# Two banded gating layers on one core: inverse roots a step later, output statistics spread over the steps, and part of the norm's columns on VectorE

## The chip, the cores and the metric

The kernel runs on one core of a Trainium2 chip. The core has TensorE (PE; PEld is its loading of weights), VectorE (DVE), ScalarE (ACT), GpSimd (POOL) and SyncE (SP), each with an instruction queue of its own that runs in order. [...] The metric is the time of one execution on the device in microseconds, median of several.

## The reference, cut to what matters

The input x is 512 x 512 positions of 64 channels. Two layers of the same form follow each other.

```python
def layer(x):
    v = gn(x)                                   # 32 groups, over all positions
    xn = ln(v)                                  # over the 64 channels
    left  = (xn @ Wl + bl) * mask * sigmoid(xn @ Wlg + blg)      # 64 -> 128
    right = (xn @ Wr + br) * mask * sigmoid(xn @ Wrg + brg)      # 64 -> 128
    gate  = sigmoid(xn @ Wog + bog)                              # 64 -> 128
    # out[i, j, h] = sum over |d| <= 4 of left[i + d, i, h] * right[i + d, j, h]
    out = banded(left, right, 4)
    out = ln(out, out_norm_scale, out_norm_bias) * gate          # over the 128 channels
    return x + out @ Wo + bo
x = layer_0(x); x = layer_1(x)
```

Everything is float32. Both layer norms need a mean and an inverse root for every one of the 262,144 positions. Two of them matter here: the norm of the input (64 channels) and the norm of the banded product, here called the output norm (128 channels).

## The kernel before, in words

**Tiling.** The rows i are cut into nine blocks of 64 rows that overlap by 8, the columns j into two halves of 256. A block and a pair of column stretches of 128 (one of each half) is a chunk, so a layer has 18 chunks. The 128 partitions hold 64 rows of one half and 64 of the other. A chunk is cut into sixteen units of eight columns (`JU = 8`, `NU = 16`), and the program advances by **steps**, one unit a step. `layer` writes out the order by hand: each engine gets its instructions in program order, step after step, and there is no planner at run time.

**What one step t issues.** In this order: the loads of later units' z tiles, the fetch of the next output unit's residual (`fetch`, tile XR), slabs of the left factor (`take_left`, tile A) and the recall of a stored transposed unit (`recall`, tile zg), all on SyncE's DMA queue; up to three output statistics; the affine of the group norm on a unit some seven to nine steps ahead (`affine`, two GpSimd instructions on z; VectorE does it for the first units of a layer); the first half of the right factor (`right`: TensorE into PSUM, sigmoid on ScalarE, product on VectorE into RO); up to two more statistics; the output gates (`gates`); the second half of `right`; the norm of the input of unit t + 2 on GpSimd (`inner_norm`, two instructions on z); `turned` (TensorE transposes of the normed output `on`, then two VectorE instructions that add a bias, multiply by the gate and write ZH); the transposes of z for unit t + 1 (`transposed`, `kept`); the bias on the residual on GpSimd (`biased`); the remaining output statistics; the input statistics of the unit whose affine was a step ago (`inner_stats`, four bn_stats); the last product with Wo, its addition to XR on VectorE and the store (`end`); in layer one sums for the next group norm; then, every fourth step, the solve; then the output norm of the next step's unit (`norm`); last the band products of the step (`mix`).

**RO.** One tile in SBUF, `[128, 64, 240, 2]`, holds the right factor and, once a `mix` has passed over it, the banded product in its place. A band product takes eight channels of a chunk (TensorE into two PSUM banks, one half copied back by ScalarE and one by VectorE). A chunk has sixteen of them, spread over ten steps, those with t % 16 from 0 to 9, one or two in each. Steps 10 to 15 have none.

**Statistics and solve.** `out_stats` is one VectorE `bn_stats` over two columns of RO; a unit has four. They can only start when the chunk's last band product is back, so from step 10 on. `looks` says at which step the four of a unit are issued, all four in the same step. In step t with `t % 4 == 3`, `solve` gathers the input statistics of four units and the output statistics of up to four: five small VectorE instructions (var, nm, a first guess of the inverse root by integer arithmetic, rs), then ten small GpSimd instructions (`rsqrt`) and two more that make the scale `rs` and the bias `nm` of the output norm. Ahead of the solve GpSimd gets the affines of the next step (`then_affine`), so that it has them to do while VectorE makes its part.

**Norm.** `norm` is eight ScalarE activations, one for each column of a unit, `on = RO * rs + nm` with a scale and a bias for each partition. The tile `on` has one buffer. The first output unit of a chunk is normed in step 13, the next in step 14 and so on, sixteen in a row.

**Buffers.** z has twelve, `ps2` (two banks each) two, `sg` two, XR four. The table `count` says how many units' affines go into each of the sixteen steps, and `ahead` follows from it; a unit's load is issued two steps before its affine, its statistics one step after.

Instructions issued through the in-order wrappers (`en.vector` and so on) all have one line in the profile, L362, so their tiles tell them apart.

Of the kernel before, what the change touches and what calls it, by code (L numbers as in the profile page):

```python
# [10 lines left out]
AF = mybir.ActivationFunctionType  # L11
ALU = mybir.AluOpType
# [10 lines left out]
JU = 8  # L23
JQ = 4
NU = JC // JU
# [54 lines left out]
def tile_two_banded_layers(  # L80
# [7 lines left out]
    _, L, _, D = x.shape  # L88
# [326 lines left out]
    def affine(u: Unit, engine):  # L415

        engine.tensor_tensor(u.z, u.z, mid(ga, JU), ALU.mult)
        engine.tensor_tensor(u.z, u.z, mid(gb, JU), ALU.add)
# [97 lines left out]
    def take_left(n: int, h: int) -> bass.AP:  # L516


        A = lp.tile([P, S, HA], F32, tag="A", name="A")
        at = n * size + h * slab + WIN * HA  # L520
        for e in range(2):
            en.sync.dma_start(
                A[e * S : (e + 1) * S].rearrange("p i h -> p (i h)"),
                strided(left_of, at, ((S + 2 * WIN) * HA, S), (1, S * HA)),
            )
        return A
# [33 lines left out]
    def out_stats(o: Out, st: bass.AP, k: int):  # L560
        en.vector.bn_stats(
            st[:, k, :],
            RO[:, :, o.c + 2 * k : o.c + 2 * k + 2, :].rearrange("p h j t -> p h t j"),
        )
# [31 lines left out]
            for n, o in enumerate(outs):  # L596
                o.rs, o.nm = ro[:, n * JU : (n + 1) * JU], nm[:, n * JU : (n + 1) * JU]

    def norm(o: Out):
        o.on = onp.tile([P, JU, H], F32, tag="on", name="on")  # L600
        for j in range(JU):
            en.scalar.activation(
                o.on[:, j, :].rearrange("p (h t) -> p h t", t=2), RO[:, :, o.c + j, :],
                AF.Identity, bias=o.nm[:, j : j + 1], scale=o.rs[:, j : j + 1],
            )

    def recall(o: Out):
        o.t = ztg.tile([P, JU // 2, P], F32, tag="zg", name="zg")
        en.sync.dma_start(o.t, later[o.at])
# [41 lines left out]
    def fetch(src: bass.AP, o: Out, w: dict, n: int):  # L651
        o.n, o.xr = n, XR[n % len(XR)]
        for e in range(2):
            en.sync.dma_start(o.xr[e * S : e * S + o.blk.m, :, 1 : 1 + 2 * D], rows_of(src, o, e))
# [38 lines left out]
    def layer(src: bass.AP, dst: bass.AP, w: dict, stats: bool, then=None):  # L693
        per = LH // JC
        n_chunks = len(blocks) * per
        LAG = NU + 14
        own = NU - JW // JU
        units, outs, lefts, mixes, looks, slabs = {}, {}, {}, {}, {}, {}
        free = NA * [NU - 2]
        for c in range(n_chunks):  # L700
            b, t0 = blocks[c // per], (c + 1) * NU
            for k in range(NU):
                t = c * NU + k
                units[t] = u = Unit(t, blk=b, j=c % per * JC + k * JU)
                j = k * JU if c % 2 == 0 else (JC + k * JU if k < own else JC - JW + (k - own) * JU)
                u.c = j

            for f in range(NU):
                o = outs[c * NU + LAG + f] = Out(
                    b, units[c * NU + (f + own) % NU], c % per * JC + f * JU  # L710
                )
                looks.setdefault(t0 + (8 + f if f > 3 else 10 + f // 2), []).append(o)

            step = [t0 + n for n, k in enumerate((2, 1, 2, 2, 1, 2, 1, 2, 2, 1)) for _ in range(k)]
            for n, t in enumerate(step):
                mixes.setdefault(t, []).append((c, n * HB))

            for h in range(H // HA):
                slabs.setdefault(free[-NA], []).append((c, h))
                free.append(step[(h + 1) * (HA // HB) - 1] + 1)  # L720
        for n in range(0, NEAR * JQ, JU):
            t = 3 + n // JU * 2
            lefts[t] = Unit(t, near=n)
        first_t, last_t = min(outs), max(outs)

        def inputs(t: int) -> list:
            return [d[t] for d in (units, lefts) if t in d]

        loads, affines, inners = {}, {}, {}
        count = [1, 1, 2, 1, 1, 1, 2, 1, 1, 1, 1, 0, 1, 1, 1, 0]
        ahead = {}
        done = -5 - NU
        for t in range(-7 - NU, n_chunks * NU):
            for _ in range(count[t % NU]):
                ahead[done + 7] = t
                done += 1
        for t in range(n_chunks * NU):
            for u in inputs(t):  # L740
                loads.setdefault(ahead[t] - 2, []).append(u)
                affines.setdefault(ahead[t], []).append(u)
                inners.setdefault(ahead[t] + 1, []).append((t, u))

        early = [u for t in sorted(loads) for u in loads[t] if u.near is None and u.at < 7]
        for u in early:
            load(src, u)
        yield
        A, sti, sto, then_affine = {}, {}, None, []
        for t in range(min(loads), last_t + 3):  # L750
            if then and t == max(units) + 2:
                then()
            for u in loads.get(t, []):
                if u not in early:
                    load(src, u)
            if t + 1 in outs:
                fetch(src, outs[t + 1], w, t + 1)
            for c, h in slabs.get(t, []):
                A[c, h] = take_left(c // per, h)
            if t + 2 in outs:  # L760
                recall(outs[t + 2])

            looking = []
            for o in looks.get(t, []):
                if sto is None:
                    sto = sm.tile([P, NB // 2, 6], F32, tag="sto", name="sto"), []
                st, os = sto
                n = len(os) * (JU // 2)
                looking += [(o, st[:, n : n + JU // 2, :], k) for k in range(JU // 2)]
                os.append(o)  # L770

            for v in looking[:3]:
                out_stats(*v)

            for u in affines.pop(t, []):
                affine(u, en.vector if u.at < NU + 4 else en.gpsimd)
            if t % 4 == 3 and t > NU:
                then_affine = affines.pop(t + 1, [])

            todo = []  # L780
            for at, u in inners.get(t, []):
                key = (at + 2) // 4
                if key not in sti:
                    sti[key] = sm.tile([P, 3 * NB // 4, 6], F32, tag="sti", name="sti", bufs=3), []
                st, us = sti[key]
                n = len(us) * (JU // 2)
                u.mean = st[:, n : n + JU // 2, 1::3]
                todo += [(u, st[:, n : n + JU // 2, :], k) for k in range(JU // 2)]
                us.append(u)

            if t in units:
                right(units[t], 0, w)
            for v in looking[3:5]:
                out_stats(*v)
            if t in outs:
                gates(outs[t], w)
            if t in units:
                right(units[t], JQ, w)
            if t in lefts:
                for q in range(0, min(JU, NEAR * JQ - lefts[t].near), JQ):  # L800
                    left(lefts[t], q, w)
            for u in inputs(t + 2):
                inner_norm(u)
            if t in outs:
                turned(outs[t], w)
            for u in inputs(t + 1):
                transposed(u)
                kept(u)
            if t in outs:
                biased(outs[t], w, stats)  # L810
            for v in looking[5:]:
                out_stats(*v)
            for v in todo:
                inner_stats(*v)
            if t - 1 in outs:
                end(dst, outs[t - 1], w)
            if stats and t - 2 in outs:
                sums(outs[t - 2], t - 2 == first_t, t - 2 == last_t)
            if t % 4 == 3:
                st, us = sti.pop((t + 5) // 4, (None, []))  # L820
                so, os = sto or (None, [])
                sto = None
                for u in then_affine:
                    affine(u, en.gpsimd)
                then_affine = []
                if us or os:
                    solve(w, us, os, st, so)
            if t + 1 in outs:
                norm(outs[t + 1])
            for n, (c, h0) in enumerate(mixes.get(t, [])):  # L830
                mix(c, A[c, h0 // HA], h0)

# [69 lines left out]
    RO = keep.tile([P, H // 2, 2 * JC - JW, 2], F32, name="RO")  # L902
# [58 lines left out]
```

## Time and profile before

| | us |
|---|---|
| median of 3 runs | 5036.04 |
| lowest, highest | 5017.72, 5038.81 |
| profiled execution, its own time | 5033.71 |
| its span, first to last instruction | 5031.9 |

| engine | busy us | share of the span |
|---|---|---|
| TensorE, products | 4211.9 | 84% |
| TensorE, weight loads | 3564.2 | 71% |
| VectorE | 3875.7 | 77% |
| ScalarE | 3636.6 | 72% |
| GpSimd | 3827.9 | 76% |

The mean granted clock of TensorE was 0.963 of full speed. The costliest single group is the output norm on ScalarE: 4608 activations `on<-RO,nm,rs`, 1868.6 us busy. The DMA queues moved 982.32 MB, 195 GB/s over the span.

How to read what follows: an instruction is named by what it writes and reads (`RO<-banks,sg`). In a timeline a row has start, length, engine, line, operation, names, shape. In a table of windows a row has the window, its length, the busy time of each engine (with the number of instructions), the granted clock, the share of busy DMA engines and GB/s. In a view by tile a row has minimum, median and maximum length in ns.

### The profile page before, as it was taken

What the parts mean: (1) busy time and instruction counts of PE and PEld (TensorE: products, weight loads), DVE (VectorE), ACT (ScalarE), POOL (GpSimd) and SP (SyncE); (2) the same over time, 40 slices, a digit from 0 to 9 for tenths busy, and PEclk for the clock granted to TensorE, in tenths of its full rate; (3) what the DMA queues carried; (4) which work ended last, traced back from release to release, by engine and by line L of the source; (5) the groups of instructions that cost most, each with busy time, mean ns of one, the idle gap of its engine ahead of it and who ended that gap; (6) DMA issues with size and microseconds to landing.
All of it is one profiled execution on the core that took longest, in us unless ns stands there. A gap on an engine that the chain in (4) does not pass through costs nothing. (4 is left out here: it accounts for less than half of the span.)

```text
span 5031.9 us, 173294 instructions
## 1 busy us (share of the span) xinstructions
PE 4211.9 (84%) x67090; PEld 3564.2 (71%) x67090; DVE 3875.7 (77%) x9661; ACT 3636.6 (72%) x8156; POOL 3827.9 (76%) x4739
## 2 busy tenths in 40 slices
PE   1026899999999999999984589999999999998998
PEld 0024788888888888888863477777777777777776
DVE  6774778888888888888766478888888888888877
ACT  0013688888888888888883268888888888888888
POOL 0036888888888888888734688888888888888863
PEclk9988999999999999999997899999999999999999
DMA  7914677767776776777663457777777777777766
GB/s 316 406 57 120 172 200 200 204 197 200 203 199 199 198 201 198 198 199 205 190 168 95 118 172 199 203 202 201 199 205 201 202 202 202 204 204 202 206 186 173
DMA packets 905343, 982.32 MB, mean 195 GB/s; under 512 B 114210, under 2 KB 641608, under 8 KB 900168
## 3 DMA queue, kind: packets, MB, share of 16 engines
q1 hardware_dynamic: 897248, 948.49, 65.2%
q10 hardware_dynamic: 7272, 22.73, 1.1%
q8 instruction: 531, 8.70, 0.8%
q14 instruction: 292, 2.39, 0.2%
HBM read 658.42 MB, written 312.46 MB: 193 GB/s over the span
## 5 line engine op out<-in xcount | busy, mean ns | idle before, releaser
L362 ACT ACTIVATE on<-RO,nm,rs 128x128 f32<-128x128 f32 x4608 | 1868.6, 495 | 13.2 <-PE bank L362 12.7
L362 PE MATMUL banks<-pack,zT 64*128 64x256 f32 x9360 | 1322.6, 404 | 128.9 <-ACT zT L362 56.2
L362 PEld LDWEIGHTS banks<-pack,zT 64*128 64x128 f32 x9360 | 884.9, 194 | 493.7 <-DVE RO L362 200.8
L362 PE MATMUL banks<-RO,A 64*64 64x128 f32 x18432 | 1169.4, 279 | 14.4 <-ACT zT L362 14.4
L362 PEld LDWEIGHTS banks<-RO,A 64*64 64x64 f32 x18432 | 1097.4, 184 | 41.3 <-ACT zT L362 17.2
L362 DVE TENSOR_TENSOR RO<-banks,sg 128x512 f32<-128x512 f32 x1152 | 787.8, 684 | 347.6 <-ACT sg L362 331.5
L362 ACT ACTIVATE sg<-banks 128x512 f32<-128x512 f32 (+1 forms) x1188 | 694.7, 587 | 364.1 <-PE banks L362 254.3
L362 DVE COPY RO<-banks 128x512 f32<-128x512 f32 x576 | 397.9, 691 | 592.8 <-ACT RO L362 592.8
L362 DVE BATCH_NORM_STATS2 sto<-RO 128x6 f32<-128x256 f32 x2304 | 847.1, 414 | 1.2
L362 DVE SCALAR_TENSOR_TENSOR ZH<-bank,pack,gate 128x448 f32<-128x448 f32 (+1 forms) x1152 | 738.7, 683 | 51.3 <-ACT gate L362 39.5
L362 POOL TENSOR_TENSOR z<-z,gb 128x512 f32<-128x512 f32 x536 | 686.6, 1281 | 42.0
L362 PE MATMUL bank<-pack,ZH 128*64 128x64 f32 x18432 | 689.4, 230 | 5.6 <-ACT gate L362 5.2
L362 POOL TENSOR_TENSOR z<-z,ga 128x512 f32<-128x512 f32 x536 | 688.5, 1284 | 0.1
L362 POOL TENSOR_TENSOR z<-z,rs 128x512 f32<-128x512 f32 x586 | 616.1, 1051 | 46.0
L362 PEld LDWEIGHTS bank<-pack,ZH 128*64 128x64 f32 x18432 | 608.0, 142 | 47.8 <-ACT gate L362 9.2
L362 POOL TENSOR_TENSOR z<-z,sti 128x512 f32<-128x512 f32 x586 | 623.1, 1063 | 0.0
L362 ACT ACTIVATE gate<-bank 128x448 f32<-128x448 f32 (+1 forms) x1152 | 566.2, 544 | 73.1 <-PE bank L362 63.0
L362 PE MATMUL bank<-zg,pack 64*128 64x448 f32 (+1 forms) x2304 | 551.7, 550 | 1.2 <-DMA zg<-later 0.8
L362 ACT COPY RO<-banks 128x512 f32<-128x512 f32 x576 | 335.7, 583 | 299.2 <-PE banks L362 299.2
L362 PEld LDWEIGHTS bank<-ident,on 64*128 64x128 f32 x9216 | 402.6, 139 | 210.1 <-ACT gate L362 97.2
L362 POOL TENSOR_TENSOR XR<-XR,pack 120x512 f32<-120x512 f32 (+1 forms) x352 | 418.7, 1191 | 135.2 <-DMA XR<-in_x_dram 50.4
L362 PE MATMUL bank<-ident,on 64*128 64x64 f32 x9216 | 443.2, 225 | 86.3 <-ACT gate L362 59.3
(140 smaller groups left out, 3756.7 us busy)
## 6 DMA issues: line engine op xcount, KB each, us to landing
later<-zT SPq DMA_DIRECT2D x576, 256.0 KB
A<-left_of SPq DMA_DIRECT2D x576, 256.0 KB
zg<-later SPq DMA_DIRECT2D x576, 256.0 KB
z<-in_x_dram SPq DMA_DIRECT2D x576, 128.0 KB
z<-mid_x SPq DMA_DIRECT2D x576, 128.0 KB
gn_x<-in_x_dram SPq DMA_DIRECT2D x16, 4096.0 KB
XR<-in_x_dram SPq DMA_DIRECT2D x448, 112.0 KB
mid_x<-XR SPq DMA_DIRECT2D x448, 112.0 KB
```

The costliest lines, as they stand in the source:

```text
L362: return lambda *a, **k: tc.keep_in_program_order(f(*a, **k))
```

## The change

Five things change, all in the order of `layer` but one.

1. `norm` takes a number of columns that VectorE does, with one `tensor_scalar` each (multiply by `rs`, add `nm`, both one value for each partition). It is 2 in steps 13 and 14 of sixteen, 3 in step 15, and 0 in the others.
2. `looks` no longer puts a unit's four output statistics into one step. Before, steps 10 to 25 (counted from a chunk's first band product) had 8, 8, 4, 4, 4, 4, then 4 in each of eight steps, and none in the last two. Now they have 5, 5, 6, 3, 3, 3, 7, then 4 in each of eight.
3. The solve comes in steps with `t % 4 == 0` and not 3. The keys that group input units go with it, and so does the early issue of the next step's affines.
4. `count`, the affines in each of sixteen steps, becomes 1, 1, 2, 1, 2, 1, 1, 2, 1, 1, 1, 0, 1, 1, 0, 0 (before: 1, 1, 2, 1, 1, 1, 2, 1, 1, 1, 1, 0, 1, 1, 1, 0), and the plan starts one unit further ahead.
5. In a layer's first sixteen steps each has one affine.

```diff
-    def norm(o: Out):
+    def norm(o: Out, on_vector: int):
+
         o.on = onp.tile([P, JU, H], F32, tag="on", name="on")
         for j in range(JU):
-            en.scalar.activation(
-                o.on[:, j, :].rearrange("p (h t) -> p h t", t=2), RO[:, :, o.c + j, :],
-                AF.Identity, bias=o.nm[:, j : j + 1], scale=o.rs[:, j : j + 1],
-            )
+            to = o.on[:, j, :].rearrange("p (h t) -> p h t", t=2)
+            of = RO[:, :, o.c + j, :]
+            nm, rs = o.nm[:, j : j + 1], o.rs[:, j : j + 1]
+            if j < JU - on_vector:
+                en.scalar.activation(to, of, AF.Identity, bias=nm, scale=rs)
+            else:
+                en.vector.tensor_scalar(to, of, rs, nm, ALU.mult, ALU.add)
...
+        look = [n for n, k in zip(range(10, 25), (5, 5, 6, 3, 3, 3, 7) + 8 * (4,)) for _ in range(k)]
...
-                looks.setdefault(t0 + (8 + f if f > 3 else 10 + f // 2), []).append(o)
+                for k in range(JU // 2):
+                    looks.setdefault(t0 + look[f * (JU // 2) + k], []).append((o, k))
...
-        count = [1, 1, 2, 1, 1, 1, 2, 1, 1, 1, 1, 0, 1, 1, 1, 0]
+        count = [1, 1, 2, 1, 2, 1, 1, 2, 1, 1, 1, 0, 1, 1, 0, 0]
         ahead = {}
-        done = -5 - NU
+        done = -4 - NU
         for t in range(-7 - NU, n_chunks * NU):
-            for _ in range(count[t % NU]):
+            for _ in range(1 if 0 <= t < NU else count[t % NU]):
                 ahead[done + 7] = t
                 done += 1
...
-            for o in looks.get(t, []):
+            for o, k in looks.get(t, []):
                 if sto is None:
                     sto = sm.tile([P, NB // 2, 6], F32, tag="sto", name="sto"), []
                 st, os = sto
-                n = len(os) * (JU // 2)
-                looking += [(o, st[:, n : n + JU // 2, :], k) for k in range(JU // 2)]
-                os.append(o)
+                if k == 0:
+                    os.append(o)
+                n = (len(os) - 1) * (JU // 2)
+                looking.append((o, st[:, n : n + JU // 2, :], k))
...
-            if t % 4 == 3 and t > NU:
+            if t % 4 == 0 and t > NU:
                 then_affine = affines.pop(t + 1, [])
...
-                key = (at + 2) // 4
+                key = (at + 1) // 4
...
-            if t % 4 == 3:
-                st, us = sti.pop((t + 5) // 4, (None, []))
+            if t % 4 == 0:
+                st, us = sti.pop((t + 4) // 4, (None, []))
...
-                norm(outs[t + 1])
+
+                norm(outs[t + 1], {13: 2, 14: 2, 15: 3}.get(t % NU, 0))
```

## The prediction

> **What bounds the kernel now.** I read the page's busy row first. No engine is full over the span, so the bound changes with the step.
>
> ```profile
> PE 4211.9 (84%) x67090; PEld 3564.2 (71%) x67090; DVE 3875.7 (77%) x9661; ACT 3636.6 (72%) x8156; POOL 3827.9 (76%) x4739
> ```
>
> Next I cut one chunk of sixteen steps at the ends of its steps: window k runs from the last ZH instruction of step k-1 to the last one of step k. These are windows 11, 12, 13, 14, 15, 0 and 1 of a chunk in layer one; the columns are length, busy time of TensorE, weight loads, VectorE, ScalarE and GpSimd, then the granted clock and DMA.
>
> ```profile
> 1502.43:1508.80 6.37, 5.66 (x96) 4.41 (x94) 6.37 (x18) 5.55 (x14) 3.69 (x3) 1.00 0.85 246
> 1508.80:1515.49 6.69, 5.32 (x94) 4.09 (x90) 6.66 (x22) 5.20 (x13) 2.86 (x10) 1.00 0.71 206
> 1515.49:1521.47 5.98, 5.54 (x98) 4.58 (x98) 4.48 (x10) 5.84 (x15) 5.67 (x8) 1.00 0.81 237
> 1521.47:1527.15 5.68, 5.23 (x95) 4.29 (x93) 5.27 (x14) 5.54 (x14) 5.52 (x6) 1.00 0.35 101
> 1527.15:1532.84 5.69, 5.25 (x96) 4.31 (x94) 5.27 (x15) 5.56 (x15) 5.53 (x6) 1.00 0.82 243
> 1532.84:1541.22 8.38, 5.13 (x70) 4.12 (x67) 8.35 (x18) 5.00 (x12) 7.33 (x14) 0.87 0.79 235
> 1541.22:1551.79 10.57, 10.57 (x188) 9.66 (x188) 5.86 (x12) 7.45 (x18) 10.18 (x12) 0.94 0.64 179
> ```
>
> See the full column of each row: VectorE in 11 and 12, ScalarE (with GpSimd) in 13, 14 and 15, VectorE in 0, TensorE in 1. Windows 2 to 10, with band products, are TensorE's (for example 7.14 busy of 7.14). Only windows 11 to 1 can gain much; over 30 chunks they average 6.4, 6.7, 6.1, 5.65, 5.6, 7.9, 10.4 us, and a chunk takes about 122 us.
>
> Why is window 0 long? The timeline at the end of step 15 shows it.
>
> ```profile
> 1410.67 1.19 POOL L362 TENSOR_TENSOR XR<-XR,fewer 120x512 f32<-120x512 f32 x1
> 1411.18 0.72 DVE L362 TENSOR_SCALAR var<-sti 128x32 f32<-128x32 f32 x1
> 1411.81 1.27 POOL L362 TENSOR_TENSOR z<-z,ga 128x512 f32<-128x512 f32 x1
> 1411.82 1.31 DVE L362 SCALAR_TENSOR_TENSOR var<-sto,pack 128x32 f32<-128x32 f32 x1
> 1413.17 0.18 DVE L362 TENSOR_SCALAR var<-var 128x32 f32<-128x32 f32 x1
> 1413.26 1.25 DVE L362 TENSOR_SCALAR nm<-sto 128x32 f32<-128x32 f32 x1
> ```
>
> The small instructions of the solve, 0.18 us elsewhere, end when a GpSimd instruction ends. Over the kernel:
>
> ```profile
> L362 DVE TENSOR_SCALAR nm<-sto x144: 167/176/1255, 538.2 to 5003.2; 128x32 f32<-128x32 f32 x144
> ```
>
> The maximum is 1.255 us against a median of 0.176. In the chunks of layer one the five solve instructions hold VectorE 2.76 us in window 0 and 0.6 us after steps 3, 7 and 11, where GpSimd already sits waiting for them. VectorE's next evacuation is late, TensorE cannot get its PSUM banks, and then runs at half clock for a while:
>
> ```profile
> 1416.30:1419.67 3.37, 3.34 (x57) 3.18 (x57) 2.64 (x5) 2.61 (x7) 2.77 (x9) 0.52 0.70 216
> 931.21:940.42 9.21, 9.21 (x162) 8.37 (x162) 5.76 (x12) 7.13 (x17) 8.57 (x13) 1.00 0.83 231
> ```
>
> The second row is a window 1 without that: 9.21 instead of 10.57 us, behind a window 0 of 7.18. Four of 30 chunks were like it.
>
> **The change, part by part.** All per chunk; 17 chunks of each of the two layers have the whole pattern, so 34.
>
> Statistics spread. One bn_stats costs VectorE 0.33 us start to start (2.63 us for the 8 of window 11). Window 11 loses three of 8: VectorE 6.37 - 1.0 = 5.4, so ScalarE's 5.55 plus what surrounds it in rows 14 and 15 (5.68) becomes the bound, a little more behind the band steps: 5.85, a gain of 0.5. Window 12 loses two of 7 and the solve of step 11 (0.6): 6.66 - 0.66 - 0.6 = 5.4, bound 5.7, gain 0.95. The statistics moved to steps 0 and 8 lie in windows that TensorE fills (VectorE 5.86 of 10.57 in window 1) and cost nothing; without that cover they are 0.33 us each.
>
> Solve a step later, after steps 0, 4, 8 and 12. Its GpSimd chain runs from 1511.88 to 1516.45 in this chunk, 4.57 us, and starts when VectorE has made rs. At step 12 VectorE first does one bn_stats (0.33) and the output addition (0.6), then the solve (0.6 to 1.1, GpSimd being about on time), so nm is ready 1.6 to 2.1 + 4.6 = 6.2 to 6.7 us after window 12 ends. The norm of step 13 needs it; ScalarE is free for it 4.5 us after that moment (it starts its norm 1 to 1.3 us ahead of the ZH end and a cycle is 5.7). So **a new wait of about 1.9 us on ScalarE** in step 13. Queued behind it are the sigmoids of step 14, and VectorE and TensorE wait for those. With two columns less (0.405 us each, 3.24 us being 8) step 14 ends about 12.9 us after window 12; window 13 stays at 6.0, so window 14 becomes 6.95: a loss of 1.25. After step 4 the wait is 0.8 to 0.9 us, of which I take 0.35 as lost through a late mix copy. After steps 0 and 8 the chain ends 8.4 and 7.5 us on, about when ScalarE asks; nothing. The solve itself leaves window 0, and lies in window 1 behind VectorE's waits.
>
> Norm columns on VectorE, 2, 2 and 3 after steps 13, 14 and 15. No such instruction is in the trace. Lower bound: 0.2 us each, from the row
>
> ```profile
> L228 DVE TENSOR_SCALAR aug<-raw,ns x2: 554/554/554, 19.0 to 54.4; 128x640 f32<-128x640 f32 x2
> ```
>
> [...] 128 elements give 0.29 us, about 0.2 start to start. Upper bound: each waits out a GpSimd instruction, 1.05 to 1.28 us. The Trainium skill ("SBUF — State Buffer", Who interferes with whom) speaks against the change: a VectorE tensor_scalar in a two-port mode and a GpSimd instruction exclude each other for the whole instruction, and whoever comes second stands still. By that rule alone two columns could cost 2 x 1.1. The trace agrees that they exclude each other (1.255 against 0.176) but shows that after one has waited the next often slips through: 2.76 - 0.6 = 2.16 us extra for four contended instructions, 0.54 each. I take **0.2 + 0.54 per column**, by that row. Is GpSimd busy then? Its own sum from step 12's solve: chain 4.6, three steps of 2.13 (norm of z) + 1.15 (bias), then 2.6 + 2.13 + 1.15 + 2.6 for step 0 (two affines, as its plan now has them): 23 us against some 26 of windows 13 to 0. It has nothing to wait for until near the end of window 0, so yes.
>
> In window 14 the two columns hide in the new ScalarE wait. Window 15 on VectorE: 5.27 - 0.33 (one bn_stats less) + 0.4 + 1.1 = 6.4, a loss of 0.7 against 5.69; ScalarE's 5.56 - 0.8 = 4.8 is no longer the bound. Window 0: five bn_stats 1.65, RO 1.2, ZH 1.25, XR 0.6, no inner statistics, three columns 0.6 + 1.6 = 6.9.
>
> Clock. The skill's page "TensorE: Matmul & The Clock Gate" (Part 1) says that idle windows of about 3.4 us halve the clock. The row here: half clock after a wait of 2.83 us in which TensorE did 0.50 us of work in 3.30; the wait of 1.4 us in window 12 left it at 1.00. By the rule neither stall need do it; by the row the first does. I go by the row: the stalls I work out for windows 14 to 0 are 1.2 to 1.9 us, so window 1 is the warm 9.2. Windows 0 and 1 together: 6.9 + 9.2 = 16.1 against 7.9 + 10.4 = 18.3, a gain of 2.2.
>
> Affines. GpSimd's work per chunk is the same (16 x (2.6 + 2.13 + 1.15) + 4 x 4.57 = 112 us, under any time here). By the plan of lead steps at most 12 z tiles live at once, before 11, and there are 12; SyncE passes step t's loads only after the output store of the step before, by when the tile is free, so its loads, XR fetches and recalls are not held. In the first 16 steps affines come evenly; I count nothing.
>
> Sum: -0.5 - 0.95 + 0 + 1.25 + 0.7 - 2.2 + 0.35 = -1.35, rounded to **-1.25 us a chunk**; 34 x 1.25 = 42. The profiled execution took 5033.7 (span 5031.9 and 1.8 around it), 2.3 below the median of 5036.0; the median becomes **4994**.
>
> **Rivals.**
> *A, the columns cost their 0.2 alone* (another access form, or GpSimd caught waiting): window 15 at 5.3 and window 0 at 5.3, total -3.9 a chunk, 4903. For it: nothing in the trace has just this form. Against: nm has strides too, and was held.
> *B, slower.* At the end of steps 14 and 15 each column waits out a whole GpSimd instruction, none slipping through. The five exposed columns cost 0.54 in my sum; the change breaks even at 0.54 + 1.25/5 = 0.8, and at 1.1 it loses 2.8 - 1.25 = 1.55 a chunk; TensorE, held as long as now in window 0, then goes to half clock again (1.3): 2.85 x 34 = 97, 5133. For it: GpSimd is continuous there. Against: var<-var passed at once above.
> *C, nothing comes of it.* The late inverse roots stall steps 13 and 5 longer (GpSimd behind at step 12) and eat the 1.35: 5036.
>
> **How the numbers follow.** My forecast 0.42, its own range 4965 to 5025; A 0.20; B 0.22; C 0.16. Half a per cent, 25 us, is about what this kernel's measurement can tell from nothing. Below 5011: most of the forecast (0.36), A, a little of C: 0.58. Within: 0.06 of the forecast, 0.10 of C: 0.16. Slower: B and the rest of C, 0.26. The range reaches to A's figure and well into B: 4895 to 5090.
>
> **What would show it.** ScalarE's norm waiting on GpSimd's nm, some 1.5 to 2.3 us a chunk; the new tensor_scalar rows at a mean near 0.8 us with a minimum near 0.29 (A: all near 0.3; B: near 1.3); windows 11 and 12 at 5.7 to 5.9, 14 near 7, 15 near 6.4; window 1 near 9.2 at clock 1.00. Wrong would be: no ScalarE wait in step 13, or half clock in window 1 as before.

## The result and the profile after

The changed kernel takes 5012.07 us (median of 7 runs, 5008.78 to 5018.52) against 5034.01 us (7 runs) for the kernel before: a ratio of 0.9959, 95% interval 0.9946 to 0.9973. It is 0.41% faster. The forecast was 4994 us, 0.84% faster; the measured time lies in its range, but the gain is half of the one forecast and, as the experiments show, partly another one.

The profiled execution has a span of 5009.3 us, 22.6 less than before. The busy row of its page:

```profile
PE 4192.2 (84%) x67090; PEld 3551.3 (71%) x67090; DVE 4032.7 (81%) x9913; ACT 3552.1 (71%) x7904; POOL 3819.7 (76%) x4739
```

ScalarE has given up 252 activations and 84 us; VectorE has taken over 252 instructions and is busy 157 us longer, 0.62 us for each, although the small instructions of its solve now take 56 us less (155.8 for 211.5). The same windows 11, 12, 13, 14, 15, 0 and 1 as in the prediction, of a typical chunk of layer one (length, busy time of TensorE, weight loads, VectorE, ScalarE, GpSimd, granted clock, DMA):

```profile
1362.29:1367.94 5.65, 5.21 (x95) 4.27 (x93) 5.58 (x15) 5.51 (x14) 5.49 (x6) 1.00 0.83 224
1367.94:1373.63 5.69, 5.23 (x94) 4.29 (x92) 5.58 (x16) 5.55 (x15) 5.53 (x6) 1.00 0.83 242
1373.63:1379.31 5.68, 5.25 (x96) 4.30 (x94) 4.99 (x16) 4.37 (x11) 4.00 (x12) 1.00 0.67 205
1379.31:1386.04 6.73, 5.24 (x94) 4.30 (x92) 6.21 (x16) 6.01 (x15) 6.50 (x8) 1.00 0.50 148
1386.04:1392.03 5.99, 4.60 (x86) 3.87 (x84) 5.99 (x14) 4.28 (x11) 5.83 (x6) 1.00 0.59 181
1392.03:1399.70 7.67, 6.08 (x112) 5.06 (x108) 7.66 (x14) 5.29 (x13) 5.99 (x6) 1.00 0.88 241
1399.70:1408.59 8.89, 8.89 (x160) 8.04 (x158) 7.03 (x19) 6.83 (x17) 5.94 (x15) 1.00 0.74 201
```

In 11 and 12 VectorE is still busy 5.58 us, but ScalarE and GpSimd now are nearly as busy (5.49 to 5.55), and the windows are about 0.7 and 1 us shorter. VectorE alone fills 15 and 0, with ScalarE at 4.28 and 5.29: the relief that the columns gave ScalarE is there and buys nothing in these two. Window 1 runs at full clock.

Step 13's norm in the timeline, the new wait:

```profile
1379.59 0.26 POOL L362 TENSOR_TENSOR nm<-nm,rs 128x32 f32<-128x32 f32 x1
1379.88 2.43 ACT L362 ACTIVATE on<-RO,nm,rs 128x128 f32<-128x128 f32 x6 [1.75 <-POOL nm L362]
```

and the start of window 0, with three columns of the norm on VectorE:

```profile
1392.28 1.05 POOL L362 TENSOR_TENSOR z<-z,sti 128x512 f32<-128x512 f32 x1
1392.65 3.04 DVE L362 TENSOR_SCALAR on<-RO,rs,nm 128x128 f32<-128x128 f32 x3
1393.42 1.04 POOL L362 TENSOR_TENSOR z<-z,rs 128x512 f32<-128x512 f32 x1
1394.42 1.18 POOL L362 TENSOR_TENSOR XR<-XR,fewer 120x512 f32<-120x512 f32 x1
1395.56 1.26 POOL L362 TENSOR_TENSOR z<-z,ga 128x512 f32<-128x512 f32 x1
```

Three columns take 3.04 us and end, at 1395.69, just behind the end of a GpSimd instruction (1395.60). In the view by tile all 252 have

```profile
L362 DVE TENSOR_SCALAR on<-RO,rs,nm x252: 333/1074/1432, 528.1 to 4938.4; 128x128 f32<-128x128 f32 x126
```

a minimum of 0.333 and a median of 1.074 us.

**Where the 22.6 us went.** Window by window, mean over the same 30 inner chunks of both traces (steps 32 to 271 of each layer); those left out differ by 0.05 or less.

| window | forecast from, to | before | after | difference |
|---|---|---|---|---|
| 11 | -0.5 | 6.38 | 5.66 | -0.72 |
| 12 | -0.95 | 6.69 | 5.64 | -1.05 |
| 13 | 0 | 6.12 | 5.65 | -0.47 |
| 14 | +1.25 | 5.65 | 6.94 | +1.29 |
| 15 | +0.7 | 5.62 | 6.16 | +0.54 |
| 0 and 1 | -2.2 | 18.25 | 16.89 | -1.36 |
| 6 | +0.35 | 8.92 | 9.85 | +0.93 |
| 4, 5, 9 | 0 | 24.63 | 24.87 | +0.24 |
| chunk | -1.25 | 121.44 | 120.72 | -0.72 |

The rest lies outside. From the trace's start or the end of layer one to the first output of a layer takes 20.4 and 13.0 us less. From the first output to the one sixteen steps on it takes 5.6 and 0.4 more, and the last 31 steps of a layer take 14.6 and 14.5 us more. So the inner chunks give 24.5 us (two times the 240 steps between these ends, where a chunk is 0.82 us shorter), the starts 33.4, and the first and last chunks take back 35.2. The prediction knew the first of the three only.

### The profile page after: what moved, and what is told of

It is laid out like the page before. It is cut to its first block, busy times and chain, and to the rows that moved or that the text cites. A ratio compares the mean times of both kernels' runs of the same rounds, so it can differ in the third digit from the quotient of the medians.

```text
span 5009.3 us, 173424 instructions
## 1 busy us (share of the span) xinstructions
PE 4192.2 (84%) x67090; PEld 3551.3 (71%) x67090; DVE 4032.7 (81%) x9913; ACT 3552.1 (71%) x7904; POOL 3819.7 (76%) x4739
## 5 line engine op out<-in xcount | busy, mean ns | idle before, releaser
L362 ACT ACTIVATE on<-RO,nm,rs 128x128 f32<-128x128 f32 x4356 | 1772.8, 496 | 131.9 <-POOL nm L362 110.8
L362 PE MATMUL banks<-pack,zT 64*128 64x256 f32 x9360 | 1317.7, 403 | 146.1 <-ACT zT L362 67.3
L362 PEld LDWEIGHTS banks<-pack,zT 64*128 64x128 f32 x9360 | 881.8, 193 | 512.4 <-DVE RO L362 216.5
L362 PE MATMUL banks<-RO,A 64*64 64x128 f32 x18432 | 1161.7, 278 | 12.8 <-ACT zT L362 12.8
L362 PEld LDWEIGHTS banks<-RO,A 64*64 64x64 f32 x18432 | 1089.7, 184 | 39.2 <-ACT zT L362 15.2
L362 DVE TENSOR_TENSOR RO<-banks,sg 128x512 f32<-128x512 f32 x1152 | 784.2, 683 | 268.9 <-ACT sg L362 250.8
L362 ACT ACTIVATE sg<-banks 128x512 f32<-128x512 f32 (+1 forms) x1188 | 694.9, 587 | 367.5 <-PE banks L362 285.0
L362 DVE BATCH_NORM_STATS2 sto<-RO 128x6 f32<-128x256 f32 x2304 | 842.3, 412 | 1.2
L362 DVE COPY RO<-banks 128x512 f32<-128x512 f32 x576 | 396.4, 691 | 503.4 <-ACT RO L362 502.9
L362 DVE SCALAR_TENSOR_TENSOR ZH<-bank,pack,gate 128x448 f32<-128x448 f32 (+1 forms) x1152 | 738.0, 682 | 61.7 <-ACT gate L362 40.6
L362 POOL TENSOR_TENSOR z<-z,gb 128x512 f32<-128x512 f32 x536 | 684.6, 1277 | 42.0
L362 POOL TENSOR_TENSOR z<-z,ga 128x512 f32<-128x512 f32 x536 | 686.1, 1280 | 0.1
L362 PE MATMUL bank<-pack,ZH 128*64 128x64 f32 x18432 | 681.5, 228 | 4.6 <-ACT gate L362 4.1
L362 POOL TENSOR_TENSOR z<-z,rs 128x512 f32<-128x512 f32 x586 | 618.6, 1056 | 45.9
L362 PEld LDWEIGHTS bank<-pack,ZH 128*64 128x64 f32 x18432 | 600.6, 141 | 45.9 <-ACT gate L362 7.4
L362 ACT ACTIVATE gate<-bank 128x448 f32<-128x448 f32 (+1 forms) x1152 | 566.5, 543 | 87.4 <-PE bank L362 76.8
L362 POOL TENSOR_TENSOR z<-z,sti 128x512 f32<-128x512 f32 x586 | 626.3, 1069 | 0.0
L362 PEld LDWEIGHTS bank<-ident,on 64*128 64x128 f32 x9216 | 409.6, 140 | 241.9 <-ACT gate L362 108.2
L362 PE MATMUL bank<-zg,pack 64*128 64x448 f32 (+1 forms) x2304 | 559.3, 556 | 4.1 <-DMA zg<-later 3.0
L362 PE MATMUL bank<-ident,on 64*128 64x64 f32 x9216 | 444.5, 227 | 124.3 <-ACT gate L362 77.3
L362 POOL TENSOR_TENSOR XR<-XR,pack 120x512 f32<-120x512 f32 (+1 forms) x352 | 418.0, 1189 | 154.5 <-DMA XR<-mid_x 54.7
L362 ACT COPY RO<-banks 128x512 f32<-128x512 f32 x576 | 332.6, 582 | 250.2 <-PE banks L362 250.1
```

The source lines that it names most:

```text
L362: return lambda *a, **k: tc.keep_in_program_order(f(*a, **k))
```

## The experiments

The theory: the inner gain is the statistics' and the moved solve's; it pays for a wait of ScalarE for the inverse roots and for columns that VectorE holds up behind GpSimd; the starts gain by the even affines, and the ends lose by the same wait. The rival: the columns are what pays, and the waits are harmless. Each ratio is to runs of the kernel before taken with that experiment, and kernels of different experiments are compared by their ratios.

**The even affines of the first sixteen steps alone,** on the kernel before.

```diff
-            for _ in range(count[t % NU]):
+            for _ in range(1 if 0 <= t < NU else count[t % NU]):
```

> The kernel before with one line of the change: in a layer's first sixteen steps each has one affine. Theory 1 (the start of each layer, where the change's trace is 20.7 us shorter from step 0 to 16 in layer one and 14.9 us in layer two, gains because SyncE waits less for free z tiles): 5034 - 35 = 4999 us, with steps 0 to 16 at about 129 and 131 us, SyncE's waits on TensorE there near 9 us and not 39, and chunks of 121.4 us as before. Theory 2 (the gain lies in the chunks and the start is only shifted work): within 8 us of 5034.

Measured: ratio 0.993 (0.9912 to 0.9948), 4990.18 against 5023.62 us, 33 us. From step 0 to 16 its layers take 129.9 and 129.3 us (before 149.4 and 145.9), its chunks 121.35. By the medians, one line of the change is worth more than the whole change (0.70% against 0.41%; the two intervals just meet). The waits of SyncE's own queue in layer one's steps 0 to 16, of the kernel before and of this one (total us, times, longest):

```profile
SPq L362 <- PE bank L362: 36.4, 7, 12.3
SPq L362 <- DVE sg L362: 11.1, 3, 6.3
```

```profile
SPq L362 <- DVE sg L362: 22.2, 4, 6.0
SPq L362 <- PE bank L362: 5.7, 2, 3.0
```

The wait on TensorE falls by 30.7 us, the one on VectorE rises by 11.1; the two together are 19.6 us less, and the stretch is 19.5 us shorter.

As I read it, SyncE stands on a z load until TensorE has transposed the unit whose tile it takes, and behind it stand the stores of zT and of the left factor, which ScalarE waits for (for the left factor's 31.7 us there, 49.5 before). With two affines in steps 2 and 6 the plan asks for up to 15 z tiles there, with one in each step for 14; there are 12. That the gain comes from the line is shown; that it comes through the z tiles was not tried apart.

**The changed kernel without columns on VectorE.**

```diff
-                norm(outs[t + 1], {13: 2, 14: 2, 15: 3}.get(t % NU, 0))
+                norm(outs[t + 1], 0)
```

> The changed kernel with all eight columns of the norm on ScalarE in every step. Theory 1 (each column on VectorE stands behind GpSimd for about 1 us): window 14 becomes 7.7 us (two columns more behind the wait for the inverse roots), window 15 5.7 and window 0 5.9 instead of 6.94, 6.16 and 7.70; in all -1.5 us a chunk, 5012 - 48 = 4964 us. Theory 2 (the columns pay: 7 x 0.405 us off ScalarE in steps that ScalarE bounds): slower, up to 5012 + 95 = 5107 us.

Measured: 0.9862 (0.9848 to 0.9877), 4955.6 us; against the change's 0.9959 the columns cost 0.97%, 49 us. Windows 14, 15 and 0 are 7.68, 6.09 and 5.66 us. The rival is refuted: seven columns of ScalarE work come back and the kernel is faster. Against the kernel with the even affines alone (0.993) what is left, the spread statistics, the moved solve and the new `count`, gains 2.35 us a chunk (no run takes these three apart): -0.72, -1.05 and -0.65 in 11 to 13, -3.56 in 0 and 1, +2.03, +0.46 and +0.99 in 14, 15 and 6.

**Columns in step 13 alone.**

```diff
-                norm(outs[t + 1], {13: 2, 14: 2, 15: 3}.get(t % NU, 0))
+                norm(outs[t + 1], {13: 2}.get(t % NU, 0))
```

> The changed kernel with columns on VectorE in step 13 alone (2 of 8). Theory 1: there VectorE's standing behind GpSimd is hidden in ScalarE's wait for the inverse roots, so window 14 stays at 6.9, window 15 goes to 5.7 and window 0 to 5.9 us: -2.3 us a chunk, 5012 - 74 = 4938 us, and about 26 below the kernel without any columns. Theory 2 (columns pay everywhere): slower than 5012 by 5 x 0.405 x 34 = 69 us.

Measured: 0.9786 (0.9772 to 0.9801), 4917.15 us, 38 us below the kernel without columns. Windows 14, 15 and 0: 6.92, 5.80, 5.66 us (7.68, 6.09, 5.66 without columns). In step 13 a column on VectorE is no faster than elsewhere (median 1.186 us); it lies in the time in which ScalarE waits for the roots. In the other two steps nothing covers it: their five columns cost 1.7%, some 87 us (0.9959 against 0.9786).

**Columns alone,** on the kernel before: its order, with `norm` of the changed kernel and the same 2, 2 and 3.

```diff
-                norm(outs[t + 1])
+                norm(outs[t + 1], {13: 2, 14: 2, 15: 3}.get(t % NU, 0))
```

> The kernel before with the columns alone (2, 2 and 3 on VectorE after steps 13, 14 and 15), everything else as before. Theory 1: without the spread statistics and with the solve still after step 15, windows 14 and 15 become about 6.9 us (before 5.65) and window 0 about 9.5 (before 7.8): +4 us a chunk, about 5034 + 140 = 5170 us. Theory 2: ScalarE's relief shows, windows 14 and 15 fall to 5.3 us, 5034 - 30 = 5004 us.

Measured: 1.0083 (1.0066 to 1.0099), 5065.35 us. The sign is theory 1's, the size isn't: +42 us, not +140. Windows 14 and 15 are 6.65 and 6.99 us, about as expected, but window 0 is 7.20 and window 1 9.42, both shorter than before (7.82 and 10.43). The view by tile shows what became free:

```profile
L362 DVE TENSOR_SCALAR on<-RO,rs,nm x252: 331/468/1425, 541.1 to 4999.5; 128x128 f32<-128x128 f32 x126
L362 DVE TENSOR_SCALAR nm<-sto x144: 172/175/189, 533.9 to 5030.9; 128x32 f32<-128x32 f32 x144
```

The maximum of nm is 0.189 us, 1.255 before. VectorE, held back in steps 13 and 14, now comes late to the solve of step 15. In the chunk whose timeline I read, its first instruction is still held (0.83 us, from 1416.10), until GpSimd's last piece of work ends at 1416.88; GpSimd then waits, and the other four take 0.18 to 0.20 us. The three columns after it run free too (their median after step 15 is 0.343 us). Which instruction is held depends on who is ahead, and one delay took away another.

**GpSimd idle beside the columns.** The changed kernel with its columns. Left out are the norm of z and the residual's bias in steps 14, 15 and 0, and the two units' affines issued in step 0.

```diff
-                affine(u, en.vector if u.at < NU + 4 else en.gpsimd)
+                if u.at < NU + 4 or t % NU != 0:
+                    affine(u, en.vector if u.at < NU + 4 else en.gpsimd)
...
             for u in inputs(t + 2):
-                inner_norm(u)
+                if t < NU or t % NU not in (14, 15, 0):
+                    inner_norm(u)
...
-            if t in outs:
+            if t in outs and t % NU not in (14, 15, 0):
                 biased(outs[t], w, stats)
...
                 for u in then_affine:
-                    affine(u, en.gpsimd)
+                    if t % NU != 0:
+                        affine(u, en.gpsimd)
```

> The changed kernel, columns on VectorE in steps 13, 14 and 15 as it has them, with GpSimd's work in steps 14, 15 and 0 left out (norm of z, bias on the residual, the affines of two units). Theory 1 (a column on VectorE is held by GpSimd's instruction): in steps 14 and 15 the columns take 0.33 us each, the median of all falls from 1.07 to about 0.35 us, window 15 goes from 6.16 to 5.3 and window 0 from 7.70 to about 5.5 us. Theory 2 (the columns are slow by themselves, through the strided read of RO): they stay near 1.07 us and the windows as they are.

```profile
L362 DVE TENSOR_SCALAR on<-RO,rs,nm x252: 329/343/1201, 528.2 to 4832.7; 128x128 f32<-128x128 f32 x126
```

The median falls from 1.074 to 0.343 us. In steps 14 and 15 no column took over 0.353; in step 13, where GpSimd still works, the median is 1.12 (1.19 with all of GpSimd's work). Windows 15 and 0 are 5.47 and 5.46 us (6.16 and 7.70). The instruction and its strided read were not slow; GpSimd was in the way. A single run took 4905.15 us.

**A shorter chain for the inverse roots,** on the kernel without columns. Left out is the second refinement; a constant replaces it.

```diff
         e.tensor_tensor(o, o, t, ALU.mult)
+        if e is not nc.vector:
+            e.tensor_scalar(o, o, 0.375, None, ALU.mult)
+            return
         e.tensor_tensor(t, o, o, ALU.mult)
```

> The changed kernel without columns on VectorE and with three instructions less in GpSimd's chain for the inverse roots (the second refinement is left out, a constant stands for it). Theory 1 (windows 14 and 6 are long because ScalarE waits for that chain): the chain is 1.1 us shorter, window 14 goes from 7.68 to about 6.6 us and window 6 from 9.91 to about 9.0: -2 us a chunk and some 10 us at the ends of the layers, from 4956 to about 4880 us. Theory 2 (window 14 is long because of VectorE's or TensorE's work, and the wait is only where ScalarE happens to stand): within 10 us of 4956.

Measured: 0.9646 (0.9627 to 0.9664), 4855.6 us; 2.2% below the kernel without columns in the same terms, where 1.5% were expected. The total of ScalarE's waits for nm, without columns:

```profile
ACT on L362 <- POOL nm L362: 109.6, 73, 3.2
```

and with the shorter chain:

```profile
ACT on L365 <- POOL nm L365: 36.3, 40, 2.1
```

(the added lines move L362 to L365). Here are windows 14, 15, 0, 1 and 6 of a chunk with the whole chain, no columns,

```profile
1484.25:1491.78 7.53, 5.24 (x70) 4.33 (x68) 4.93 (x13) 6.36 (x16) 7.29 (x9) 0.83 0.52 153
1491.78:1498.29 6.51, 6.51 (x123) 5.71 (x122) 4.94 (x13) 6.21 (x16) 6.31 (x6) 0.93 0.58 175
1498.29:1503.97 5.68, 5.21 (x96) 4.28 (x94) 4.79 (x11) 5.54 (x14) 4.74 (x4) 1.00 0.67 209
1503.97:1512.89 8.92, 8.92 (x160) 8.07 (x158) 7.02 (x19) 6.88 (x17) 5.97 (x15) 1.00 0.82 230
1545.09:1554.73 9.64, 9.08 (x162) 8.17 (x162) 7.45 (x20) 7.98 (x19) 9.40 (x9) 1.00 0.90 249
```

and with the short one:

```profile
1466.99:1473.45 6.46, 5.23 (x94) 4.29 (x92) 4.93 (x13) 6.32 (x17) 6.30 (x7) 1.00 0.46 138
1473.45:1479.14 5.69, 5.24 (x94) 4.29 (x92) 4.94 (x14) 5.55 (x15) 5.53 (x6) 1.00 0.72 209
1479.14:1484.84 5.70, 5.24 (x96) 4.32 (x94) 4.80 (x12) 5.56 (x15) 4.77 (x5) 1.00 0.76 216
1484.84:1493.75 8.91, 8.91 (x160) 8.07 (x158) 7.01 (x19) 6.86 (x17) 6.97 (x14) 1.00 0.77 215
1525.94:1534.94 9.00, 9.00 (x160) 8.15 (x160) 7.34 (x20) 6.98 (x17) 8.77 (x9) 1.00 0.91 251
```

Windows 14 and 6 lose 1.06 and 1.00 us in the mean of 30 chunks, close to the 1.03 us by which the chain is shorter (median 4.56, now 3.53). Windows 15 and 5 are 0.36 and 0.27 shorter too, which I had not expected: some 19 us of the extra gain. In window 15 the rows show the clock: 0.83 and 0.93 in the first two rows with the whole chain, 1.00 with the short one. GpSimd also does 12 instructions less a chunk here, and how much of the gain is that was not tried apart.

**The ends of the layers put back, columns in step 13.** In the last chunk of a layer the statistics and the solve stand where the kernel before has them.

```diff
+                    if c == n_chunks - 1:
+                        at = 8 + f if f > 3 else 10 + f // 2
...
-            if t % 4 == 0:
+            if t % 4 == (3 if t > n_chunks * NU + 8 else 0):
                 st, us = sti.pop((t + 4) // 4, (None, []))
```

> The changed kernel with columns on VectorE in step 13 alone, and the last chunk of each layer with statistics and solve where the kernel before has them. Theory 1 (with no units left a step takes 4.1 us and the chain of 6.5 us, one step ahead, makes ScalarE wait every fourth step; two steps ahead it doesn't): the last sixteen steps of each layer go back from 77 and 71 us to about 68 and 61, 4917 - 18 = 4899 us. Theory 2 (the end of the layers is longer for another reason): 4917 within 6 us.

Measured: 0.9727 (0.9706 to 0.9748), 4901.14 us, 2.7% faster than the kernel before and, through it, 2.3% faster than the changed one and 0.6% faster than the one with columns in step 13 alone. The last 15 steps take 68.3 and 60.1 us (before 68.4 and 60.5; changed 77.8 and 72.2). It leaves nothing out and is faster than both kernels.

## Why the prediction was half right

**Statistics spread, windows 11 and 12:** right, 1.77 us for 1.45, and another 0.47 in window 13 that I had put at nothing. No run has the spread without the moved solve, so the share of each is not shown, nor why window 13 is shorter.

**The wait for the inverse roots in step 13:** right in place and size. ScalarE waits 1.75 us in the chunk shown and 1.78 in the mean of 30 (1.9 forecast), window 14 grew by 1.29 (1.25). The shorter chain shows the cause: 1.03 us off it took 1.06 off window 14.

**The same wait in step 5:** the mechanism was right and the size of the loss wrong. The wait is what I worked out (0.93 us in the mean of 30 chunks for 0.8 to 0.9), but I took only 0.35 of it as lost, and window 6 lost 0.93, the whole of it; the shorter chain gives all of it back. That is some 0.6 us in each of 34 chunks, 20 us.

**Columns on VectorE:** the mechanism was right and the term was too small in window 0. I took 0.74 us a column, from four instructions of which some slip through. The two columns after step 14 take just that (mean 0.73), and window 15 came out near my figure (+0.54 for +0.7). The three after step 15 hold VectorE 3.02 us in the mean of the inner chunks, 1.0 each, nearer to what the rule of the Trainium skill ("SBUF — State Buffer", Who interferes with whom) gives when each stands for a whole GpSimd instruction (1.05 to 1.3). With 3.0 in place of 2.2 my own sum for window 0 becomes 7.7, and 7.70 was measured. Windows 0 and 1 gained 1.36 and not 2.2 us, and the difference is this term.

**The clock in window 1:** the number was right and the step to it wrong. The mean of window 1 is 9.19 us for 10.43, as forecast. I had gone by the length of the stall, and by that all chunks should have full clock; 21 of the 30 in the table have it (3 before; the prediction's 4 are counted from a chunk later on). In the other nine the granted clock is 0.85 to 0.95, in five of them behind a window 0 of 7.65 to 7.67 us, as long as in most of the 21. The changed kernel's trace shows more. All its half-clock stretches in the chunks begin on one grid of cells of 3.41 us. Here are two cells in a row of a chunk with a window 0 of 7.66 us and a slow window 1, and then two of the chunk shown above:

```profile
788.04:791.46 3.42, 1.84 (x44) 1.52 (x43) 3.42 (x8) 1.30 (x3) 3.17 (x3) 1.00 0.48 135
791.46:794.87 3.41, 3.41 (x54) 3.29 (x51) 3.21 (x11) 3.27 (x9) 0.09 (x1) 0.50 0.76 236
```

```profile
1392.20:1395.62 3.42, 3.34 (x42) 2.56 (x37) 3.42 (x5) 3.17 (x8) 3.34 (x5) 1.00 0.94 246
1395.62:1399.03 3.41, 1.90 (x52) 1.72 (x54) 3.41 (x10) 1.29 (x4) 2.47 (x2) 1.00 0.84 232
```

In the cell ahead of each of the 19 such stretches TensorE was busy 1.3 to 2.0 us; of the cells that no half clock followed, the least busy had 1.82. So in this trace the half clock goes with the work in one cell, and with where a stall falls on the grid, not with the length of the stall. It is no sharp threshold: in the kernel without columns the two ranges overlap more (1.1 to 2.3, and 1.45). That 21 chunks came out warm is in part luck.

**The sum of the inner chunk:** -0.72 and not -1.25 us. Windows 0 and 1 (0.84 short), 6 (0.58) and 4, 5 and 9 (0.24) are the losses against the working; 11 to 13 (0.79 more than forecast) and 15 (0.16) the gains.

**What was missing:** the step "In the first 16 steps affines come evenly; I count nothing" failed. It is worth 33 us, shown by the run with that line alone. The other omission is its opposite: I multiplied the inner chunk by 34 and never looked at the steps after the last unit. There a step takes 4.55 us in layer one and 4.03 in layer two before the change, with nothing but the norm and the gates on ScalarE, and a chain that is ready 6.5 us later, one step ahead, is late every fourth step; the last 31 steps of the layers took 29 us more, and putting back the old order in the last chunk gives 20 back. That both signs came out near each other is luck.

**Rivals.** A (columns at their own 0.2) is about what happens when GpSimd is out of the way, and only then: three columns take 0.86 us, 0.29 each, and windows 15 and 0 are 5.47 and 5.46 us (5.3 by A). B named the right mechanism, with a price between mine and its own in step 15. C, that nothing comes of it, fell by its number; its reason was partly right, as the waits in step 5 and at the ends cost more than I gave them.

## What to carry to other kernels

Work moved to an engine pays by the time that it takes there beside its neighbours, not by its time alone: here 0.34 us became 1 us beside a busy GpSimd, and the move paid only where another wait covered it. A plan of steps has a beginning and an end with other bounds than its middle; work out each of a change's lines for all three. And a chain of small dependent instructions (a dozen in 4.56 us) needs its lead in time and not in steps: one step of 9 us is enough here, one of 7.0, 5.7 or 4.0 to 4.6 is not.

## What I had not expected of the hardware

Delays can cancel: columns put in front of a contended solve removed its contention (nm at most 0.189 us for 1.255) because GpSimd had gone idle by then, as the one timeline that I read shows it. A VectorE tensor_scalar beside a GpSimd that never pauses is not held for a fixed time: of the columns after step 15 some took 0.335 us and some up to 1.432, in a row of three about 1 us each. And a wait of some 2 us for the inverse roots went with a granted clock of 0.83 in window 14 of the chunk shown, 1.00 where it was 1 us shorter.
